# Attention and mixture of experts on one core: the order inside a group of value products, when inverses are read, how the groups are cut

## The chip, the cores and the metric

The kernel runs on one core of one Trainium2 chip. Its metric is the device time of one execution in microseconds (us). TensorE (PE) multiplies and transposes into PSUM, VectorE (DVE) and ScalarE (ACT) compute on SBUF and PSUM, GpSimd (POOL) and SyncE (SP) issue most of the DMA transfers. Each engine takes its own instructions in order; semaphores join them.

## The reference

One transformer layer on 2048 tokens of width 128: attention with 16 heads of width 64 under a causal mask, then a feed-forward part with one shared and eight routed experts, two of them for each token.

```python
x = x + attention(layernorm(x), qkv_w, qkv_b, out_w, out_b)
x = x + ffn(layernorm(x), gate_w, experts..., shared...)

# attention
qkv = einsum('bse,ehd->bshd', x, qkv_w) + qkv_b
q, k, v = split(qkv, 3)
logits = where(mask, einsum('bqhd,bkhd->bhqk', q, k) / sqrt(64), -0.7 * max)
probs = softmax(logits)
out = einsum('bhqd,hde->bqe', einsum('bhqk,bkhd->bqhd', probs, v), out_w) + out_b
```

Everything is fp32. The change lies in the attention part, which takes about the first 870 us of the profile.

## The kernel before

**Units of work.** The tokens are 16 blocks of 128. Heads are taken two at a time: eight pairs `j`. For each pair the query blocks are taken two at a time: eight values of `m`, in the order `turns = [2, 7, 0, 6, 1, 5, 3, 4]` (line 384). A step is one `(j, m)`; there are 64. Step `m` covers the query blocks 2m and 2m+1, here called rows 2m and 2m+1, and the key blocks 0 to 2m+1.

**Scores** (`score_units`, line 394). A row is worked in units of 512 keys: PE makes the scores of both heads into two PSUM tiles (line 429), DVE scales them, or adds the mask on the last unit, writes them to SBUF and takes the maximum on the way (lines 440 and 444: the eviction). After the last unit of a row DVE makes the negated maximum (`neg`), ACT takes the exponential of the row in place and its sum, once for each head (line 461). A row of m = 7 has four units, of m = 6 four, of m = 5 and 4 three, of m = 3 and 2 two, of m = 1 and 0 one. Scores are made ahead: a step with m >= 4 makes those of the step four places later, another step those of the step two places later.

**Turning the probabilities.** The value product needs the probabilities with keys on the partitions. For m < 4 PE transposes each 128x128 block (`turn`, line 522) and ACT copies it out of PSUM to `pT` (line 525). For m >= 4, called near steps in the code (`by_slabs(m)` is their number of key blocks turned this way), only the last two or four key blocks go that way, into `tail` (`turn_last`); the rest goes by slabs: DVE transposes a whole row of one head in 32x32 squares (line 496, 1536 columns for m = 7 and 6, 1024 for m = 5 and 4), SP issues four DMAs that write it to a DRAM buffer `stage` (line 500), and when all four slabs of the step are there one DMA reads the 3 or 2 MB back as `turned` (`load_turned`, line 514).

**One buffer for the rows of near steps.** The two rows of every near step, q = 0 and q = 1, lie in two SBUF tiles with one buffer each (line 413: the tag is `row7_0` or `row7_1`, `bufs=1`). So the first eviction of row 10 waits until everything has read row 12, its forerunner in the same tile: the exponentials, the transposes of `turn_last`, the slab transposes and the `stage` DMAs. The rows of q = 0 follow each other as 14, 12, 10, 8, those of q = 1 as 15, 13, 11, 9, round after round.

**When slabs and inverses are done.** After a row's exponentials, two entries (one a head) go into the queue `to_turn` with an age of 2 (line 464). Each group of work below begins with `turn_slabs(1)`, which lowers every age by one and does at most one slab if the first entry's age is below zero; later in the group `turn_slabs(1, age=False, due=True)` does one more that is due. When the last entry of a row is taken, DVE takes the reciprocals of the sums (line 480); when both rows of a step are through, it transposes them (line 483) and POOL writes them to DRAM (`invd`, line 485). `load_turned` does first whatever slabs of its step are left.

**Values and projection.** `times_v` (line 554) accumulates the value product of both heads over the key blocks in one of two PSUM tiles `av`; `spread` reads the inverses back over 64 partitions each (`inb`, line 567, four issues by POOL); `divide` multiplies the two on DVE into `aT` (line 575); `project` multiplies by the output weights on PE (`po`, line 581) and DVE adds to the residual `xr` (line 582).

**The loop** (lines 665 to 730). Each step is cut in groups of key blocks: a near step in its tail and two halves of the slab part, another step in threes (m = 3: 3, 3, 2; m = 2: 3, 3; m = 1: 3, 1; m = 0: 2). A group of a step with m < 4 is: one unit of `fill` (the next pair's projections, lines 352 and 369), slabs, the turns of this group (in the first group `spread` too), the projection of a finished step, the value products of the group before, `divide` if they end a step, slabs that are due, score units. A near group is the same with its own value products at once and `fill` after them. The score units of a near step with six or eight units are put as 3, 3, rest behind its three groups. There are 20 groups a pair. In the last pair the same loop also moves the routing of the feed-forward part on, one piece a group (`route_on`).

**What sets the order.** PE and DVE keep the order of the program text (`manual_schedule`). The order on ACT, POOL and SP is made by the scheduler. PSUM has six buffers with the tag `r`, used in turn by scores (two a unit), transposes, projections and `fill`, and two for `av`.

## Time and profile before

| what | value |
|---|---|
| median of 3 runs | 1049.83 us (1049.36 to 1052.5) |
| the profiled execution | 1043.9 us, span 1042.2 us |
| mean granted TensorE clock | 0.971 |
| PE busy | 949.6 us, 91% of the span |
| DVE busy | 745.1 us, 71% |
| ACT busy | 541.3 us, 52% |
| POOL busy | 211.3 us, 20% |
| HBM traffic | 105.10 MB read, 99.35 MB written |
| `stage` DMAs of a 1536-column slab | 192 KB each, four a slab, median 3.8 us to landing |
| `turned` DMA of m = 7 and 6 | 3072 KB, median 10.7 us to landing |

The profile is of one execution. A busy share is an average over stages; matmul ends are modelled, so a long matmul entry can hold a wait. In a timeline line the columns are start (us from the span's start), length in us, engine, source line, operation, tiles, shapes, count, and in brackets the idle time of the engine before it and what ended it. In a table of windows each line is a stretch of time, its length, the busy time (and instruction count) of PE, weight loads, DVE, ACT and POOL in it, the granted TensorE clock, the mean busy share of the DMA engines and GB/s.

### The profile page before, as it was taken

What the parts mean: (1) busy time and instruction counts of PE and PEld (TensorE: products, weight loads), DVE (VectorE), ACT (ScalarE), POOL (GpSimd) and SP (SyncE); (2) the same over time, 40 slices, a digit from 0 to 9 for tenths busy, and PEclk for the clock granted to TensorE, in tenths of its full rate; (3) what the DMA queues carried; (4) which work ended last, traced back from release to release, by engine and by line L of the source; (5) the groups of instructions that cost most, each with busy time, mean ns of one, the idle gap of its engine ahead of it and who ended that gap; (6) DMA issues with size and microseconds to landing.
All of it is one profiled execution on the core that took longest, in us unless ns stands there. A gap on an engine that the chain in (4) does not pass through costs nothing. (4 is left out here: it accounts for less than half of the span.)

```text
span 1042.2 us, 18362 instructions
## 1 busy us (share of the span) xinstructions
PE 949.6 (91%) x5928; PEld 573.3 (55%) x5928; DVE 745.1 (71%) x2315; ACT 541.3 (52%) x1015; POOL 211.3 (20%) x404
## 2 busy tenths in 40 slices
PE   4987999999999999999999999999999788689995
PEld 2553545565556556555555555556555446357773
DVE  3764788778877877887778777876787675545553
ACT  4552546655655565456556554655465452315551
POOL 1030110121102111111111111111111112734441
PEclk9988999999999999999999999999999898889998
DMA  9996748774787478747866875677577751443104
GB/s 200 190 275 172 272 117 308 251 215 144 258 277 213 160 245 272 210 165 252 257 189 190 253 245 174 204 250 243 165 221 254 250 172 65 142 129 85 43 26 125
DMA packets 126736, 205.33 MB, mean 197 GB/s; under 512 B 16449, under 2 KB 119203, under 8 KB 122545
## 3 DMA queue, kind: packets, MB, share of 16 engines
q1 hardware_dynamic: 116496, 190.06, 59.9%
q0 software_dynamic: 8416, 13.82, 5.4%
q8 instruction: 48, 0.79, 0.3%
q10 hardware_dynamic: 1728, 0.27, 0.2%
q14 instruction: 48, 0.39, 0.1%
HBM read 105.10 MB, written 99.35 MB: 196 GB/s over the span
## 5 line engine op out<-in xcount | busy, mean ns | idle before, releaser
L461 ACT ACTIVATE row<-row,neg 128x1920 f32<-128x1920 f32 (+15 forms) x256 | 306.3, 1202 | 255.0 <-DVE neg L458 115.2
L440 DVE TENSOR_SCALAR_CACHE_REDUCE row<-sc 128x512 f32<-128x512 f32 x384 | 243.2, 684 | 97.9 <-PE sc L429 68.2
L429 PE MATMUL sc<-kT,qT 64*128 64x512 f32 (+3 forms) x1280 | 299.4, 557 | 14.1 <-DVE row L440 5.9
L429 PEld LDWEIGHTS sc<-kT,qT 64*128 64x128 f32 x1280 | 128.3, 188 | 149.9 <-issue 79.9
L496 DVE STREAM_TRANSPOSE row<-row 128x1024 f32<-128x1024 f32 (+1 forms) x128 | 190.3, 1490 | 0.8 <-ACT row L461 0.8
L554 PE MATMUL av<-turned,vt 128*64 128x256 f32 x1280 | 158.0, 395 | 0.0
L485 POOL DMA_DIRECT2D invd<-inv x64 | 46.0, 718 | 506.3 <-DVE inv L483 503.1
L444 DVE CUSTOM_DVE_ANT_0 row<-sc,mask 128x384 f32<-128x384 f32 (+3 forms) x256 | 114.8, 485 | 19.6 <-PE sc L429 19.0
L554 PEld LDWEIGHTS av<-turned,vt 128*64 128x64 f32 x1280 | 88.7, 140 | 63.5 <-issue 24.6
L522 PE MATMUL tr<-ident,row 128*128 128x128 f32 x896 | 119.2, 276 | 3.3 <-ACT pT L525 1.9
L522 PEld LDWEIGHTS tr<-ident,row 128*128 128x128 f32 x896 | 99.6, 141 | 36.3 <-issue 19.0
L567 POOL DMA_DIRECT2D inb<-invd x128 | 76.1, 603 | 146.0 <-DMA invd<-inv 133.4
L525 ACT COPY pT<-tr 128x512 f32<-128x512 f32 (+1 forms) x160 | 79.0, 553 | 31.9 <-PE tr L522 31.9
L554 PE MATMUL av<-pT,vt 128*64 128x256 f32 (+1 forms) x640 | 79.6, 372 | 6.4 <-ACT pT L525 6.1
L352 PE MATMUL pq<-xnT,wq 128*128 128x512 f32 x128 | 72.0, 650 | 2.4 <-DVE row L440 2.4
L581 PE MATMUL po<-wo,aT 128*128 128x128 f32 x256 | 44.2, 297 | 26.0 <-DVE row L440 19.7
L554 PEld LDWEIGHTS av<-pT,vt 128*64 128x64 f32 x640 | 38.7, 136 | 47.9 <-issue 18.3
L581 PEld LDWEIGHTS po<-wo,aT 128*128 128x128 f32 x256 | 34.7, 197 | 44.1 <-DVE row L440 36.3
L525 ACT COPY tail<-tr 128x512 f32<-128x512 f32 x96 | 43.6, 520 | 16.7 <-PE tr L522 16.7
L949 POOL DMA_INDIRECT ybuf<-yo,to x39 | 38.3, 982 | 62.2 <-ACT yo L948 59.1
L461 ACT ACTIVATION_READ_ACCUMULATOR row<-row,neg 128x1 f32 x256 | 49.7, 194 | 0.0
L575 DVE TENSOR_TENSOR aT<-av,inb 128x256 f32<-128x256 f32 x64 | 26.5, 415 | 27.5 <-DMA inb<-invd 15.2
(169 smaller groups left out, 894.9 us busy)
## 6 DMA issues: line engine op xcount, KB each, us to landing
stage<-row SPq DMA_DIRECT2D x256, 192.0 KB, 3.8
turned<-stage SPq DMA_DIRECT2D x16, 3072.0 KB, 10.7
stage<-row SPq DMA_DIRECT2D x256, 128.0 KB, 2.6
turned<-stage SPq DMA_DIRECT2D x16, 2048.0 KB, 8.8
zbuf<-mask SPq DMA_DIRECT2D x8, 1056.0 KB, 19.2
inb<-invd POOLq DMA_DIRECT2D x128, 64.0 KB, 3.4
zs<-zbuf SPq DMA_DIRECT2D x39, 66.0 KB, 1.9
yt<-ybuf SPq DMA_DIRECT2D x4, 512.0 KB, 4.3
```

Of the source, the lines that this page charges most:

```text
L352: nc.tensor.matmul(pq, wq_of[j][:, s, :, :], xnT[:, ts(n, 512)], start=True, stop=True,)
L429: nc.tensor.matmul(sc[:, :cw], qT[i // 4][hd, ts(i % 4, P)], keys, start=True, stop=True)
L440: nc.vector.tensor_scalar(dst, src, SCALE, None, ALU.mult, ALU.max, accum_out=mh)
L444: nc.vector.tensor_tensor_reduce(out=rows[:, h, c0 : c0 + cw], in0=scs[h][:, :cw], in1=mask[:, 512 - cw : 512], scale=SCALE, scalar=-F32_M ...
L461: nc.scalar.activation(row, row, AF.Exp, bias=neg[:, h : h + 1], accum_out=sums[:, h : h + 1])
L485: nc.gpsimd.dma_start(invd_of[j, m].rearrange("n (a i) -> a n i", a=4), inv,)
L496: nc.vector.transpose(row, row)
L522: nc.tensor.transpose(tr[:, h, ts(q, P)], rows_of[j, m][q][:, h, ts(b, P)], ident)
L525: nc.scalar.copy(dst[:, :, q0 * P :], tr[:, :, q0 * P :])
L554: nc.tensor.matmul(av_of[j, m][hd, q0 * P :], vt[:, b, hd], pT[:, h], start=(b == near), stop=(b == (near or 2 * m + 2) - 1),)
L567: nc.gpsimd.dma_start(inb[h * D : (h + 1) * D, :].rearrange("d (q p) -> d q p", q=2), row.partition_broadcast(D),)
L581: nc.tensor.matmul(po[:, q, :], aT[:, ts(q, P)], wo[:, j, :], start=True, stop=True)
```

## The change

Five things are changed together.

1. The loop goes over a flat list of groups. A group now begins with its own value products; the turns of a group with m < 4 are made one group earlier, behind the value products of that group. The order inside is: slabs, (projection of a finished step if this group ends a step), value products, `divide` or else the projection, routing, due slabs, the next group's turns, one `fill` unit, `spread` of the next step, tails, `load_turned`, scores.
2. `spread` is put one group earlier, at the end of the step before. Rows of steps with m < 4 enter `to_turn` with age 1 instead of 2, and taking such an entry no longer counts against the one slab.
3. m = 2 is one group of six blocks, m = 3 two of four, m = 1 two of two: 18 groups a pair instead of 20.
4. Score units of a near step are put as 3, rest, 3 behind its three groups; a step of two groups has half behind each.
5. In the routing of the last pair the transposes of all its rows are one piece instead of one piece for each four.

No instruction's shape and no count of them changes. In the built program the DVE order around the step m = 7 of a pair is now: evictions of rows 0 and 1, slab of row 12, `xr` of m = 2, slab of row 12, eviction of row 10, two slabs of row 13, inverses of m = 6 and m = 0, `aT` of m = 7, eviction of row 11, slab of row 10. Before it was: two slabs of row 12, evictions of rows 0 and 1, slab of row 13, `aT` of m = 2, inverses of m = 6, slab of row 13, eviction of row 10, `xr` of m = 2, eviction of row 11, inverses of m = 0, `aT` of m = 7, slab of row 10.

```diff
--- before.py
+++ after.py
@@ -335,8 +335,11 @@
                     )
                     no_order("sent", ins)
 
-        turns = [lambda t0=t0: turn_row(t0) for t0 in range(0, n, 4)]
-        return [statistics, normed, None, *turns, None, logits, None, best1, best2, ranks]
+        def turn_rows():
+            for t0 in range(0, n, 4):
+                turn_row(t0)
+
+        return [statistics, normed, None, turn_rows, None, logits, None, best1, best2, ranks]
 
 
     attn = tc.tile_pool(name="attn", bufs=2)
@@ -461,7 +464,7 @@
                     nc.scalar.activation(
                         row, row, AF.Exp, bias=neg[:, h : h + 1], accum_out=sums[:, h : h + 1]
                     )
-                to_turn.extend([j, m, q, h, sums, 2] for h in range(2))
+                to_turn.extend([j, m, q, h, sums, 2 if X else 1] for h in range(2))
 
             units += [lambda c=c, unit=unit: unit(c) for c in range(nch)]
         return units
@@ -473,7 +476,9 @@
 
         for t in to_turn:
             t[-1] -= age
-        while to_turn and (to_turn[0][-1] < 0 or not (age or due)) and most:
+        while to_turn and (to_turn[0][-1] < 0 or not (age or due)):
+            if not most and by_slabs(to_turn[0][1]):
+                break
             j, m, q, h, sums, _ = to_turn.popleft()
             if h == 1:
                 inv = inv_of[j, m]
@@ -625,7 +630,6 @@
         u()
         turn_slabs(2)
     fill, later = deque(), deque()
-    last = []
     ending = None
 
     shared_w = []
@@ -662,73 +666,91 @@
                     blocks = [b for m in batch for b in (2 * m, 2 * m + 1)]
                     routes.append(deque(route_units(blocks)))
 
-    for n, (j, m) in enumerate(steps):
+    def groups_of(m):
+
+        near, width = by_slabs(m), 2 * m + 2
+        if near:
+            return [range(near, width), range(near // 2), range(near // 2, near)]
+        step = {2: 2, 4: 2, 6: 6, 8: 4}[width]
+        return [range(k, k + step) for k in range(0, width, step)]
+
+    def runs_of(m, units):
+
+        if by_slabs(m):
+            return [3, units - 6, 3]
+        return [units] if m in (0, 2) else [units // 2, units // 2]
+
+    groups = [(n, k, g) for n, (_, m) in enumerate(steps) for k, g in enumerate(groups_of(m))]
+
+    def turned_group(i):
+        n, _, group = groups[i]
+        return [turned(*steps[n], b) for b in group]
+
+    now = turned_group(0)
+    spread(*steps[0])
+    for i, (n, k, group) in enumerate(groups):
+        j, m = steps[n]
+        near = by_slabs(m)
         at = n % NM
-        if at == 0 and j + 1 < NP:
-            qkv[j + 1] = qkv_units(j + 1)
-
-
-            _, q, k, v = qkv[j + 1]
-            fill.extend([*k, q[3], *v])
-            later.extend([q[1], q[0], q[2]])
-            if j + 2 < NP:
-                load_wq(j + 2, nc.sync)
-            while j and blank:
-                nc.sync.dma_start(blank.popleft(), mask[:, :ROW].unsqueeze(1).to_broadcast([P, 16, ROW]))
-        if at == 0 and j == NP - 1:
-            load_shared()
-        if at == 5 and later:
-            assert not fill
-            fill.extend(later)
-            later.clear()
-        if at == 6 and j + 1 < NP:
-            assert not fill
-        near = by_slabs(m)
-        coming = scores_of(n + (4 if near else 2))
+        if k == 0:
+            if at == 0 and j + 1 < NP:
+                qkv[j + 1] = qkv_units(j + 1)
+
+
+                _, q, key, v = qkv[j + 1]
+                fill.extend([*key, q[3], *v])
+                later.extend([q[1], q[0], q[2]])
+                if j + 2 < NP:
+                    load_wq(j + 2, nc.sync)
+                while j and blank:
+                    clear = mask[:, :ROW].unsqueeze(1).to_broadcast([P, 16, ROW])
+                    nc.sync.dma_start(blank.popleft(), clear)
+            if at == 0 and j == NP - 1:
+                load_shared()
+            if at == 5 and later:
+                assert not fill
+                fill.extend(later)
+                later.clear()
+            if at == 6 and j + 1 < NP:
+                assert not fill
+            coming = scores_of(n + (4 if near else 2))
+            runs = runs_of(m, len(coming))
+            if n == 0:
+                coming.extend(scores_of(3))
+                runs = [len(coming)]
+        turn_slabs(1)
+
+        before, ending = ending, None
+        ends = group[-1] == (near or 2 * m + 2) - 1
+        if before is not None and ends:
+            finish(*before)
+        for t in now if not near else turned_group(i):
+            times_v(*t, qkv[j][0][2])
+        if ends:
+            ending = (j, m, divide(j, m))
+        elif before is not None:
+            finish(*before)
+        route_on()
+        turn_slabs(1, age=False, due=True)
+        if i + 1 < len(groups) and not by_slabs(steps[groups[i + 1][0]][1]):
+            now = turned_group(i + 1)
+        if fill:
+            fill.popleft()()
+        if i + 1 < len(groups) and groups[i + 1][1] == 0:
+            spread(*steps[n + 1])
+        if near and k == 0 and n + 2 < len(steps):
+            turn_last(*steps[n + 2])
+        if n == 0 and k == 0:
+            turn_last(*steps[1])
         if n == 0:
-            coming.extend(scores_of(3))
-
-        if near:
-            groups = [list(range(near, 2 * m + 2))]
-            groups += [list(range(k, k + near // 2)) for k in range(0, near, near // 2)]
-            runs = [3, 3, len(coming) - 6]
-        else:
-            groups = [list(range(k, min(k + 3, 2 * m + 2))) for k in range(0, 2 * m + 2, 3)]
-            half = len(coming) // 2
-            runs = {1: [len(coming)], 2: [2 * (half // 2), half], 3: [0, half, half]}[len(groups)]
-        for k, group in enumerate(groups):
-            if fill and not near:
-                fill.popleft()()
-            turn_slabs(1)
-            now = [turned(j, m, b) for b in group]
-            if k == 0:
-                spread(j, m)
-            if ending is not None:
-                finish(*ending)
-                ending = None
-            route_on()
-            ready, last = (last + now, []) if near else (last, now)
-            for t in ready:
-                jt, mt, b = t[:3]
-                times_v(*t, qkv[jt][0][2])
-                if b == (by_slabs(mt) or 2 * mt + 2) - 1:
-                    assert ending is None
-                    ending = (jt, mt, divide(jt, mt))
-            if fill and near:
-                fill.popleft()()
-            turn_slabs(1, age=False, due=True)
-            if near and k == 0 and n + 2 < len(steps):
-                turn_last(*steps[n + 2])
-            if n == 0 and k == 0:
-                turn_last(*steps[1])
-            if n == 0 and k == 1:
-                load_turned(*steps[1])
-            if near and k == 1 and n + 2 < len(steps):
-                load_turned(*steps[n + 2])
-            for _ in range(runs[k] if k < len(groups) - 1 else len(coming)):
-                if coming:
-                    coming.popleft()()
-    assert not last
+            load_turned(*steps[1])
+        if near and k == 1 and n + 2 < len(steps):
+            load_turned(*steps[n + 2])
+        for _ in range(runs[k]):
+            if coming:
+                coming.popleft()()
+        if k == len(runs) - 1:
+            assert not coming
     finish(*ending)
     assert len(routes) == 2
     attn.__exit__(None, None, None)
```

## The prediction

> **What bounds the kernel now.** I read the page's busy table first, then stretches of one pair in the table of windows, then the timelines of DVE and PE where two stretches that do the same work differ in length.
>
> ```profile
> PE 949.6 (91%) x5928; PEld 573.3 (55%) x5928; DVE 745.1 (71%) x2315; ACT 541.3 (52%) x1015; POOL 211.3 (20%) x404
> ```
>
> PE is the bound on the whole. From one pair to the next it takes about 101.4 us (slabs of row 14 start at 357.77 and 459.13), and DVE's instructions for a pair add up to some 84 us of that, so DVE may idle 17 us a pair before it binds. But a pair does not always run at PE's pace. The next table holds the same work twice, from the tail products of m = 7 to the scores behind the first group of m = 6: in the first pair, and in the fourth.
>
> ```profile
> 75.00:117.00 42.00, 32.17 (x186) 17.85 (x183) 25.97 (x65) 18.16 (x32) 4.93 (x10) 0.92 0.74 240
> 390.00:420.00 30.00, 28.76 (x190) 17.67 (x186) 23.05 (x62) 15.71 (x34) 4.79 (x9) 1.00 0.81 260
> ```
>
> The work is the same to a few instructions, the time 42 against 30 us. Cut in fives, the first pair shows why: DVE does nothing at all in two of the slices, while the DMA engines are at 0.95 and 0.91.
>
> ```profile
> 75.00:80.00 5.00, 3.96 (x30) 2.31 (x28) 4.38 (x10) 4.59 (x6) 0.73 (x1) 1.00 0.95 397
> 80.00:85.00 5.00, 2.22 (x12) 0.78 (x8) 0.00 (x0) 0.38 (x2) 1.32 (x3) 1.00 0.95 276
> 85.00:90.00 5.00, 2.54 (x12) 1.75 (x14) 3.30 (x11) 0.00 (x0) 0.00 (x0) 0.68 0.13 46
> 90.00:95.00 5.00, 5.00 (x24) 2.25 (x21) 4.30 (x8) 3.02 (x5) 0.73 (x1) 0.63 0.33 69
> 95.00:100.00 5.00, 5.00 (x34) 2.58 (x36) 0.00 (x0) 0.68 (x1) 0.12 (x1) 1.00 0.91 242
> ```
>
> DVE's timeline of that pair names the wait: the slab of row 12 ends, and the eviction of row 10, which goes into the same SBUF tile, idles 7.25 us until the slab's DMAs have landed; then row 13 and row 11 do it again.
>
> ```profile
> 77.70 1.75 DVE L496 STREAM_TRANSPOSE row<-row 128x1536 f32<-128x1536 f32 x1
> 86.70 0.69 DVE L440 TENSOR_SCALAR_CACHE_REDUCE row<-sc 128x512 f32<-128x512 f32 x1 [7.25 <-DMA stage<-row]
> ...
> 92.63 1.74 DVE L496 STREAM_TRANSPOSE row<-row 128x1536 f32<-128x1536 f32 x1
> 101.13 0.69 DVE L440 TENSOR_SCALAR_CACHE_REDUCE row<-sc 128x512 f32<-128x512 f32 x1 [6.76 <-DMA stage<-row]
> ```
>
> In the fourth pair the same distance, 387.25 to 395.23, is 7.98 us, but DVE fills it with rows 0 and 1, the slabs of row 13 and a division, and idles 0.85 us:
>
> ```profile
> 385.50 1.75 DVE L496 STREAM_TRANSPOSE row<-row 128x1536 f32<-128x1536 f32 x1
> 390.00 1.77 DVE L496 STREAM_TRANSPOSE row<-row 128x1536 f32<-128x1536 f32 x1
> 395.23 0.69 DVE L440 TENSOR_SCALAR_CACHE_REDUCE row<-sc 128x512 f32<-128x512 f32 x1 [0.85 <-DMA stage<-row]
> 401.71 0.69 DVE L440 TENSOR_SCALAR_CACHE_REDUCE row<-sc 128x512 f32<-128x512 f32 x1 [2.46 <-PE sc L429]
> ```
>
> PE shows what that is worth to the end. In the first pair it idles because the six PSUM tiles hold scores that DVE has not read.
>
> ```profile
> 75.00 1.68 PE L554 MATMUL av<-tail,vt 128*64 128x256 f32 x16
> 87.46 1.23 PE L581 MATMUL po<-wo,aT 128*128 128x128 f32 x4 [5.24 <-DVE row L440]
> 88.61 5.29 PE L554 MATMUL av<-turned,vt 128*64 128x256 f32 x24
> ...
> 116.72 0.71 PE L581 MATMUL po<-wo,aT 128*128 128x128 f32 x4 [0.48 <-DVE row L440]
> ```
>
> ```profile
> 390.22 1.68 PE L554 MATMUL av<-tail,vt 128*64 128x256 f32 x16
> 396.75 2.81 PE L554 MATMUL av<-turned,vt 128*64 128x256 f32 x24
> 419.39 0.71 PE L581 MATMUL po<-wo,aT 128*128 128x128 f32 x4 [1.24 <-DVE row L440]
> ```
>
> From the tail products to the last projection: 116.72 - 75.00 = 41.72 us against 419.39 - 390.22 = 29.17 us, 12.55 us apart.
>
> **The change, part by part.** I work against the profiled execution's own 1043.9 us; the median of the runs, 1049.83, is 0.6% above it.
>
> *Six blocks in one group, scores as 3, rest, 3.* Ages fall once a group. Row 12 is finished behind the second group of m = 4. Before, four groups followed until row 10's eviction (third of m = 4, two of m = 2, first of m = 7) and its slabs came due in the second of m = 2. Now m = 2 is one group, so they come due in the first group of m = 7, and in DVE's order nothing but row 12's own slab stands right ahead of row 10. Row 13's two slabs come behind row 10, and ahead of row 11 stand only two inverses and one division (0.7 us). That is the first pair's pattern, now in every pair. DVE's chain from the start of row 12's first slab: slab, `xr`, slab 3.75 us; wait 7.25; row 10 3.6 (86.70 to 90.31); two slabs 3.7; wait 6.76 (the inverses inside it); row 11 3.8: 28.9 us. In the fourth pair it took 21.9 us (383.77 to 405.66) and began 6.4 us ahead of the tail products; now it begins about 1 us behind them, once the evictions of rows 0 and 1 are through. So row 11 is out of PSUM about 30 us after the tail products begin, not 15.4. PE meanwhile has 17.4 us of work until it needs a tile of row 11 (products of m = 7, 7.2 us; six score units, 5; projection, turns, `fill`, 5.2) and waits for the rest. What follows row 11 (slabs of row 10, rows 2, 3 and 8, tails of m = 5) took 11.8 us in the first pair. Bounds: row 11's scores now stand one group later than in the first pair, which could hide one run of products with its turns, 3.6 us, so from below 8.9; from above, row 12's transfers meet the 3 MB read of m = 7 (10.5 us from issue to landing at 375.16) and the inverses of m = 0 come late as well, 17. I take 12.5 us, the nearest row. It counts for pairs two to seven, 6 x 12.5 = 75. The first pair pays already. The last pair paid 31.4 us for this stretch (795.22 to 826.67), with 6.07 us of DVE idle for the inverses of m = 0; it goes to about 41.5, +10.
>
> *Rows 14 and 15 to rows 12 and 13.* m = 3 has two groups instead of three, so these slabs come nearer to their successors too. All sixteen stage DMAs took 17 us from the first slab (357.77) to the last landing; DVE has about 15 us of work in between. New wait 1 to 2.5 us a pair on DVE, partly behind PE's products.
>
> *Values first, turns behind them.* Removed: PE's wait for the copies `pT` (0.98 us once a pair at m = 2, 6.1 us in the windows 100 to 800) and part of its waits at a projection, which no longer stands right behind three score units except in m = 0 and m = 2 (7.4 us in the same window). Added: the last four blocks of m = 3 are copied by ACT behind row 15's exponentials (2.02 + 2.00 us, then 2.0 us of copies); from row 15's scores on, ACT needs about 10.1 us and PE 8.2, so PE waits about 2 us a pair. The six copies of m = 2 stand behind row 12's exponentials (2 x 1.68), another 0.8. With the item above I take +1.5 us a pair over the rest of the pair, bounds -4 (all six microseconds of stalls there go, nothing comes but half the ACT wait) and +5: 7 x 1.5, about +10.
>
> *Inverses a step ahead.* In the steady pairs DVE waited about 2 us for `inb` of m = 0 (9.1 us in five waits), because `invd` was issued at 406.35 behind the `turned` read of 401.46. Now it goes out with that of m = 6, before the read; but the division follows in its own group. POOL is 20% busy and its four issues take 2.4 us; nothing else waits behind them. Gain at most 2 us a pair, inside a stretch that the chain above sets: 0. On SP the stage DMAs of row 12 now stand behind the read of m = 7, which waits for row 15's landing first; SP has been free of it by then (10 us): 0, and in the upper bound above.
>
> *Routing in ten pieces, 18 groups in the last pair.* The same pieces end in the same group; one more piece of the second batch is done in the loop: -1 (0 to -3).
>
> Sum: 1043.9 + 75 + 10 + 10 - 1 = 1138.
>
> The granted clock after such a wait: 0.68 and 0.63 in the windows 85 to 95, and 24 value products took 5.29 us instead of 2.81. In the first pair that loss lies inside DVE's chain, so it is 0 in my sum. [...]
>
> **The rivals.**
> *Faster.* The wait is covered: PE runs ahead into `av`, which has its own PSUM tiles, and the gains remain (0.98 + 1 + 2 us a pair): 1043.9 - 7 x 4 = 1016. It decides this way if DVE idles less than about 2 us ahead of row 10. Against it stands DVE's order and the 5.24 us that PE lost in the first pair.
> *Half.* DVE waits, but PE's lost time is only about 6 us a pair, since one of the two waits is covered by the later place of row 11's scores and the other gains come in: 1044 + 7 x 6 = 1086.
> *Worse.* Transfers are the bound: stage, `turned` and `inb` meet, 17 to 18 us a pair: 1044 + 7 x 18 = 1170.
> *No change.* What the order gives and takes cancels: 1044 to 1050.
>
> **How the numbers follow.** My case 0.71, half 0.12, worse 0.12, faster 0.04, no change 0.01. Time 1140. The range, 1088 to 1175, holds my own case with both ends of its bounds and about half of the two cases beside it; what is left out are the cases of 0.05 at the fast end and the outer halves of the others. Faster by over 0.3%, about what a measurement of this kernel can tell, 0.04; within it 0.01; slower 0.95.
>
> **What would show it.** Right: DVE's wait `row <- DMA stage<-row` grows from 27.0 us to over 100 us; ahead of row 10 it idles 6 to 8 us in each pair; the pair lasts 113 to 117 us; PE idles ahead of the `fill` unit between the value halves of m = 7 and ahead of the projection of m = 7; HBM traffic is unchanged. `av <- ACT pT` waits move from m = 2 to m = 3. Wrong: if slabs of row 12 end more than 8 us before row 10's first eviction, or if PE has idled under 5 us where DVE waited 14.

## The result, and the profile after

The changed kernel takes 1178.36 us (median of 4 runs, 1176.81 to 1180.09); the kernel before, timed beside it, 1050.87. The ratio is 1.121 (95% interval 1.119 to 1.124). The forecast was 1140 with 1088 to 1175: right in sign and in its main mechanism, too low by 38 us, and the result lies 3 us beyond its range. The runs timed beside each other are 127.5 us apart; the profiled execution took 1177.42 us (span 1175.7), 133.5 us above the one before.

Where these 133.5 us lie is read from the PE timelines. I cut each pair at two places that stand in both kernels: the first tail product of m = 7, and the first product of m = 6 on the slab part. From the one to the other is "the stretch", from there to the next pair's tail products "the rest". The "first expert product" is PE's first work on an expert's block (`pz`). The forecast column has the prediction's terms.

| part of the run | before, us | after, us | difference | forecast |
|---|---|---|---|---|
| start to the first pair's tail products | 75.0 | 72.7 | -2.3 | 0 |
| pair 1: stretch + rest | 42.4 + 71.7 | 43.6 + 76.2 | +5.8 | +1.5 |
| pairs 2 to 7: stretch | 176.9 | 244.0 | +67.1 | +75 |
| pairs 2 to 7: rest | 429.3 | 465.4 | +36.1 | +9 |
| last pair, tail products of m = 7 to the last projection | 84.7 | 100.9 | +16.2 | +10 |
| last projection to the first expert product | 46.8 | 60.4 | +13.6 | -1 |
| experts to the end | 115.5 | 112.4 | -3.1 | 0 |

The busy table of the page, whose columns are as in the line shown of the kernel before:

```profile
PE 998.2 (85%) x5928; PEld 598.2 (51%) x5928; DVE 739.6 (63%) x2315; ACT 545.9 (46%) x1017; POOL 211.9 (18%) x404
```

No engine has more to do; PE's busy time is 49 us longer for the same 5928 products, at a mean granted clock of 0.939 instead of 0.971. The waits of the whole run (engine, line, what was waited for: us in total, times, longest) point at the cause; in the kernel before the first of these lines stood at 27.0 us in 7 waits, the second at 19.7 in 10:

```profile
DVE row L443 <- DMA stage<-row: 178.0, 35, 7.6
...
PE po L586 <- DVE row L443: 54.8, 15, 9.9
...
PE pq L355 <- DVE row L443: 24.5, 8, 4.0
```

DVE's timeline of the fourth pair shows where these waits stand:

```profile
432.72 1.75 DVE L501 STREAM_TRANSPOSE row<-row 128x1536 f32<-128x1536 f32 x1
440.80 0.69 DVE L443 TENSOR_SCALAR_CACHE_REDUCE row<-sc 128x512 f32<-128x512 f32 x1 [6.33 <-DMA stage<-row]
...
446.38 1.74 DVE L501 STREAM_TRANSPOSE row<-row 128x1536 f32<-128x1536 f32 x1
...
455.09 0.69 DVE L443 TENSOR_SCALAR_CACHE_REDUCE row<-sc 128x512 f32<-128x512 f32 x1 [6.18 <-DMA stage<-row]
...
460.82 1.22 DVE L501 STREAM_TRANSPOSE row<-row 128x1024 f32<-128x1024 f32 x1
...
470.72 0.69 DVE L443 TENSOR_SCALAR_CACHE_REDUCE row<-sc 128x512 f32<-128x512 f32 x1 [5.16 <-DMA stage<-row]
...
475.23 1.21 DVE L501 STREAM_TRANSPOSE row<-row 128x1024 f32<-128x1024 f32 x1
...
482.27 0.69 DVE L443 TENSOR_SCALAR_CACHE_REDUCE row<-sc 128x512 f32<-128x512 f32 x1 [5.16 <-DMA stage<-row]
```

Each pair of lines is a row's last slab and the first eviction into the same SBUF tile: row 12 and row 10, 13 and 11, 10 and 8, 11 and 9. The first two are what the prediction described; in the kernel before the same place idled 0.85 us. The other two, 5.16 us each, it had not priced. PE in the stretch of this pair:

```profile
434.86 2.81 PE L559 MATMUL av<-turned,vt 128*64 128x256 f32 x24
441.55 2.08 PE L355 MATMUL pq<-xnT,wq 128*128 128x512 f32 x2 [3.88 <-DVE row L443]
443.56 4.88 PE L559 MATMUL av<-turned,vt 128*64 128x256 f32 x24
...
455.85 0.71 PE L586 MATMUL po<-wo,aT 128*128 128x128 f32 x4 [2.96 <-DVE row L443]
```

and in the table of windows (start:end, length, busy time of PE, weight loads, DVE, ACT and POOL, granted clock, DMA share, GB/s):

```profile
433.48:438.48 5.00, 4.19 (x32) 2.02 (x28) 0.99 (x1) 0.00 (x0) 0.00 (x0) 1.00 0.93 233
438.48:443.48 5.00, 1.93 (x2) 0.50 (x2) 2.68 (x9) 0.00 (x0) 0.00 (x0) 0.75 0.25 73
443.48:448.48 5.00, 5.00 (x26) 2.69 (x26) 4.89 (x12) 3.70 (x5) 0.73 (x1) 0.57 0.27 58
448.48:453.48 5.00, 4.40 (x20) 1.87 (x20) 0.42 (x1) 1.55 (x3) 0.82 (x2) 1.00 0.94 236
453.48:458.48 5.00, 2.63 (x16) 1.44 (x18) 3.39 (x11) 0.00 (x0) 2.53 (x5) 1.00 0.70 213
```

This is the picture that the prediction drew from the first pair: DVE stands still twice while the DMA engines are at 0.93 and 0.94, and PE idles ahead of the `fill` unit and of the projection of m = 7. After the idle of 3.88 us the granted clock was 0.75 and 0.57 and 24 products took 4.88 us instead of 2.81; after that of 2.96 us it stayed at 1.00.

In the rest of this pair PE waited as follows, first in the kernel before (420.03:491.58, 71.55 us), then in the kernel after (469.33:547.39, 78.06 us):

```profile
PE av L554 <- ACT pT L525: 1.0, 1, 1.0
PE sc L429 <- ACT tail L525: 0.7, 1, 0.7
PE tr L522 <- ACT pT L525: 0.2, 1, 0.2
```

```profile
PE po L586 <- DVE row L443: 1.8, 1, 1.8
PE tr L527 <- ACT pT L530: 1.2, 1, 1.2
PE pq L355 <- ACT pT L530: 1.1, 1, 1.1
PE sc L432 <- DVE xr L587: 0.9, 1, 0.9
PE sc L432 <- DVE row L443: 0.8, 1, 0.8
PE pv L372 <- DVE row L443: 0.2, 1, 0.2
```

The waits for ACT's copies grow from 1.9 to 2.3 us, those for DVE from nothing to 3.7. The remaining 2.4 us stand inside PE's own entries, 71.92 us instead of 69.56 at a granted clock of 1.00 in both; a modelled entry can hold a wait, and the trace doesn't say for what.

### The profile page after: what moved, and what is told of

It reads as the page before. It is cut to its first block, busy times and chain, and to the rows that moved or that the text cites. A ratio compares the mean times of both kernels' runs of the same rounds, so it can differ in the third digit from the quotient of the medians.

```text
span 1175.7 us, 18345 instructions
## 1 busy us (share of the span) xinstructions
PE 998.2 (85%) x5928; PEld 598.2 (51%) x5928; DVE 739.6 (63%) x2315; ACT 545.9 (46%) x1017; POOL 211.9 (18%) x404
## 3 DMA queue, kind: packets, MB, share of 16 engines
HBM read 105.10 MB, written 99.35 MB: 174 GB/s over the span
## 5 line engine op out<-in xcount | busy, mean ns | idle before, releaser
L443 DVE TENSOR_SCALAR_CACHE_REDUCE row<-sc 128x512 f32<-128x512 f32 x384 | 243.0, 685 | 242.3 <-DMA stage<-row 178.0
L432 PE MATMUL sc<-kT,qT 64*128 64x512 f32 (+3 forms) x1280 | 319.1, 573 | 25.0 <-DVE row L443 11.2
L432 PEld LDWEIGHTS sc<-kT,qT 64*128 64x128 f32 x1280 | 142.7, 192 | 169.1 <-issue 51.0
L559 PEld LDWEIGHTS av<-turned,vt 128*64 128x64 f32 x1280 | 89.4, 141 | 77.1 <-issue 34.3
L355 PE MATMUL pq<-xnT,wq 128*128 128x512 f32 x128 | 79.0, 709 | 32.2 <-DVE row L443 24.5
L530 ACT COPY pT<-tr 128x512 f32<-128x512 f32 (+1 forms) x160 | 75.3, 547 | 65.2 <-PE tr L527 65.1
L586 PE MATMUL po<-wo,aT 128*128 128x128 f32 x256 | 49.7, 321 | 56.0 <-DVE row L443 54.8
L559 PEld LDWEIGHTS av<-pT,vt 128*64 128x64 f32 x640 | 42.5, 144 | 36.9 <-issue 17.4
L367 ACT ACTIVATE kT<-pq,bqk 128x512 f32<-128x512 f32 x32 | 21.7, 681 | 72.1 <-PE pq L355 72.0
```

The source lines that it names most:

```text
L355: nc.tensor.matmul(pq, wq_of[j][:, s, :, :], xnT[:, ts(n, 512)], start=True, stop=True,)
L432: nc.tensor.matmul(sc[:, :cw], qT[i // 4][hd, ts(i % 4, P)], keys, start=True, stop=True)
L443: nc.vector.tensor_scalar(dst, src, SCALE, None, ALU.mult, ALU.max, accum_out=mh)
L530: nc.scalar.copy(dst[:, :, q0 * P :], tr[:, :, q0 * P :])
L559: nc.tensor.matmul(av_of[j, m][hd, q0 * P :], vt[:, b, hd], pT[:, h], start=(b == near), stop=(b == (near or 2 * m + 2) - 1),)
L586: nc.tensor.matmul(po[:, q, :], aT[:, ts(q, P)], wo[:, j, :], start=True, stop=True)
```

## The experiments

All kernels compute the whole reference. Stretch and rest are means over pairs two to six; "wait" is DVE's wait `row <- DMA stage<-row` in the whole run; "routing" is the time from the last projection to the first expert product. The runs were made in five sets, each on one chip with its own runs of the kernel before (medians 1052.8, 1042.0, 1053.5, 1042.9 and 1043.6), so times are compared as ratios or pair by pair. Of each diff the lines that carry the experiment are shown; some also move the first `turned` read or the score units to fit the new groups.

| set | kernel | median, us | ratio to before (95%) | stretch | rest | wait | routing |
|---|---|---|---|---|---|---|---|
| - | before, profiled | 1043.9 | 1 | 29.4 | 71.9 | 27.0 | 46.8 |
| - | after | 1178.4 | 1.121 (1.119 to 1.124) | 40.7 | 77.5 | 178.0 | 60.4 |
| 1 | a_early | 1090.7 | 1.038 (1.031 to 1.046) | 31.4 | 75.5 | 29.4 | 60.3 |
| 1 | a_33 | 1127.7 | 1.072 (1.064 to 1.079) | 33.5 | 78.1 | 37.3 | 60.0 |
| 1 | a_sc33 | 1178.5 | 1.120 (1.113 to 1.127) | 41.4 | 77.9 | 123.3 | 60.7 |
| 1 | b_six | 1152.2 | 1.095 (1.088 to 1.102) | 41.4 | 75.2 | 97.5 | 59.1 |
| 2 | a_early33 | 1078.0 | 1.035 (1.032 to 1.037) | 28.9 | 77.1 | 41.1 | 47.8 |
| 2 | a_early_m3 | 1108.5 | 1.063 (1.060 to 1.066) | 31.7 | 78.9 | 24.7 | 46.4 |
| 2 | b_early | 1045.9 | 1.003 (1.002 to 1.005) | 29.1 | 73.0 | 25.8 | 45.6 |
| 2 | a_pad | 1163.5 | 1.117 (1.114 to 1.120) | 40.6 | 77.6 | 177.6 | 47.7 |
| 3 | b_late | 1212.1 | 1.150 (1.143 to 1.156) | 46.8 | 75.7 | 184.9 | 59.9 |
| 3 | b_inv | 1039.4 | 0.987 (0.982 to 0.992) | 28.3 | 71.2 | 25.9 | 60.6 |
| 3 | b_sc | 1049.3 | 0.996 (0.993 to 0.998) | 29.4 | 71.1 | 53.6 | 56.2 |
| 3 | a_33sc33 | 1130.6 | 1.074 (1.068 to 1.080) | 33.0 | 78.9 | 39.0 | 60.0 |
| 4 | b_all | 1136.8 | 1.088 (1.083 to 1.092) | 39.0 | 77.2 | 141.5 | 46.4 |
| 4 | a_early33sc33 | 1076.6 | 1.031 (1.028 to 1.035) | 30.6 | 74.9 | 18.5 | 47.7 |
| 4 | b_inv_pad | 1025.0 | 0.982 (0.979 to 0.986) | 28.2 | 71.2 | 24.9 | 45.7 |
| 4 | b_inv_sc_pad | 1034.2 | 0.991 (0.987 to 0.994) | 29.4 | 71.0 | 42.5 | 45.7 |
| 5 | b_inv2 | 1027.9 | 0.985 (0.982 to 0.988) | 28.3 | 71.2 | 28.7 | 46.9 |
| 5 | b_inv_pad2 | 1024.8 | 0.983 (0.980 to 0.985) | 28.1 | 71.2 | 23.9 | 45.7 |

### Is it the nearness of slab and eviction?

**a_early**, the kernel after with slabs one group earlier:

```diff
-                to_turn.extend([j, m, q, h, sums, 2 if X else 1] for h in range(2))
+                to_turn.extend([j, m, q, h, sums, 1] for h in range(2))
```

> The kernel after with one number changed: slabs of the near rows come due one group of turns earlier (age 1, not 2), everything else as it is. In VectorE's order row 12's slabs then stand ahead of the evictions of rows 0 and 1 and row 13's slabs, as in the kernel before, instead of right ahead of row 10's eviction. Theory (the time is set by evictions that wait for the landing of a slab they follow too closely, in the stretch of m = 7 and again ahead of rows 8 and 9): the wait row <- DMA stage<-row falls from 178 us to under 60, and both parts of the loss go, the 11 us a pair in the stretch and most of the 6 us in the rest: 1040 to 1070 us. Rival A (the rest of a pair is lost to the values-first order itself, ScalarE's copies behind the exponentials): only the stretch comes back, 7 x 11 us and the last pair's 8: about 1085 to 1095. Rival B (the transfers are the bound, whatever the order): the wait moves to another reader of the same bytes and the time stays above 1150.

Measured 1.038. The wait is back at 29.4 us with the same bytes moved, so rival B, transfers as the bound, falls. DVE around row 10 in the fourth pair:

```profile
402.92 1.75 DVE L501 STREAM_TRANSPOSE row<-row 128x1536 f32<-128x1536 f32 x1
...
406.06 1.77 DVE L501 STREAM_TRANSPOSE row<-row 128x1536 f32<-128x1536 f32 x1
...
408.37 1.74 DVE L501 STREAM_TRANSPOSE row<-row 128x1536 f32<-128x1536 f32 x1
410.94 0.69 DVE L443 TENSOR_SCALAR_CACHE_REDUCE row<-sc 128x512 f32<-128x512 f32 x1 [0.83 <-DMA stage<-row]
```

From the end of row 12's last slab to row 10's eviction it is still 6.3 us (404.67 to 410.94), but DVE fills them with two evictions and the slabs of row 13. The stretch is back at 31.4 us, but the rest only went from 77.5 to 75.5: the time is what rival A had forecast. Something besides these waits costs 3.6 us a pair there. (Beside the 2 us that are left in the stretch stands a wait of DVE of 3.09 us for `inb`; in the kernel before it was 1.97 us.)

**b_late**, the kernel before with slabs one group later. PE's order is the same, instruction for instruction:

```diff
-                to_turn.extend([j, m, q, h, sums, 2] for h in range(2))
+                to_turn.extend([j, m, q, h, sums, 3] for h in range(2))
```

> The kernel before with one number changed: slabs come due one group of turns later (age 3, not 2). The order of the work on PE is the same, instruction for instruction; only VectorE's order moves: row 12's slabs stand right ahead of row 10's eviction, row 13's ahead of row 11's, row 10's ahead of row 8's, row 11's ahead of row 9's, as in the kernel after. Theory (this nearness alone, with none of the change's parts, makes the loss): the stretch of m = 7 goes from 29.8 to 41 or 42 us in pairs two to seven and to 42 in the last, the rest of a pair from 71.5 to 73 to 75; the wait row <- DMA stage<-row to 130 to 180 us: 1044 + 6 x 12 + 10 + 7 x 2.5 = about 1143, 1125 to 1165. Rival (the nearness costs only together with fewer groups or values first): under 1080.

Measured 1.150, more than the theory's 1.08 to 1.12 and more than the whole change. DVE in its fourth pair:

```profile
442.58 1.76 DVE L496 STREAM_TRANSPOSE row<-row 128x1536 f32<-128x1536 f32 x1
450.52 0.69 DVE L440 TENSOR_SCALAR_CACHE_REDUCE row<-sc 128x512 f32<-128x512 f32 x1 [6.18 <-DMA stage<-row]
...
456.43 1.74 DVE L496 STREAM_TRANSPOSE row<-row 128x1536 f32<-128x1536 f32 x1
464.51 0.69 DVE L440 TENSOR_SCALAR_CACHE_REDUCE row<-sc 128x512 f32<-128x512 f32 x1 [6.35 <-DMA stage<-row]
```

So nearness, with no part of the change, makes a loss of this kind. It isn't quite nearness alone: the excess over the theory lies in the stretch, 46.8 instead of 42 us, for the edit delays the inverses too, and DVE waited 5.48 us for the `inb` of m = 0 there.

**b_early**, the other side of it: the same line of the kernel before with age 1.

```diff
-                to_turn.extend([j, m, q, h, sums, 2] for h in range(2))
+                to_turn.extend([j, m, q, h, sums, 1] for h in range(2))
```

> The kernel before with the slabs (and inverses) due one group of turns earlier, nothing else. Theory: in its steady pairs no eviction waits for a landing, so there is little to gain; the waits that it has, 27 us in 7 times, lie in the first pair and the last: -6 to +3 us against the kernel before. Rival (earlier slabs meet VectorE's other work or the exponentials that they need, and cost): +1 to +2 us a pair, 8 to 16 us slower. If the time of the kernel before is also set by the nearness of slabs, over 10 us faster.

Measured 1.003, 3.9 us slower. One group earlier gains nothing, one group later costs 15%: the kernel before stood just inside the edge.

### Which part of the change brings it about?

**b_six**, the kernel before with only the six blocks in one group:

```diff
-            groups = [list(range(k, min(k + 3, 2 * m + 2))) for k in range(0, 2 * m + 2, 3)]
+            size = 6 if m == 2 else 3
+            groups = [list(range(k, min(k + size, 2 * m + 2))) for k in range(0, 2 * m + 2, size)]
```

> The kernel before with one part of the change alone: the six blocks of m = 2 in one group (19 groups a pair instead of 20), the old order within a group, the old cut of the scores. VectorE's order then has row 12's slabs right ahead of row 10's eviction and row 13's slabs ahead of row 11's, as in the kernel after; rows 8 and 9 keep the order of the kernel before. Theory: the stretch of m = 7 grows by 10 to 13 us in pairs two to seven and by 8 to 10 in the last, and the rest of a pair stays at 71.5 us: 1050 + 6 x 11 + 8 = 1115 to 1135. Rival (the stretch is lost only together with the values-first order): under 1080.

Measured 1152, above the range. The stretch is 12.0 us longer, as the theory has it; the rest did not stay at 71.5 but went to 75.2. A wait of only 97.5 us (after: 178.0) costs four fifths of the whole loss.

All 16 of these waits stand ahead of rows 10 and 11; no eviction of row 8 or 9 waits. What lengthens the rest here is read from PE at the cut, in the fourth pair:

```profile
461.49 1.22 PE L581 MATMUL po<-wo,aT 128*128 128x128 f32 x4 [3.24 <-DVE row L440]
462.65 4.92 PE L554 MATMUL av<-turned,vt 128*64 128x256 f32 x24
```

```profile
460.75:465.75 5.00, 4.26 (x20) 2.71 (x22) 3.43 (x15) 1.78 (x3) 0.12 (x1) 0.50 0.49 112
```

PE idled 3.24 us at the end of the stretch, the granted clock fell to 0.50, and the first 24 products of the rest took 4.92 us instead of 2.81. In pairs two to seven they took 4.46 to 5.16 us, so 1.7 to 2.4 of the 3.3 us that the rest is longer stand in these slow products. Shortly ahead of that idle DVE had waited 3.96 us for the `inb` of m = 0.

**a_33**, the other way round: the kernel after with m = 2 in two groups of three.

```diff
-        step = {2: 2, 4: 2, 6: 6, 8: 4}[width]
+        step = {2: 2, 4: 2, 6: 3, 8: 4}[width]
```

(and the scores of rows 0 and 1 cut as before)

> The kernel after with m = 2 in two groups of three blocks again (scores of rows 0 and 1 cut as before, 2 units and the rest), nothing else undone: 19 groups a pair. Row 12's slabs get one group more ahead of row 10's eviction; rows 10 and 8 keep theirs (row 8's eviction still follows row 10's slabs by one group, row 9's follows row 11's). Theory: the wait of some 6.3 us ahead of row 10 goes, those ahead of row 11 shrinks by the overlap, those of about 5 us ahead of rows 8 and 9 stay: 6 to 9 us a pair back of the 17, so 1115 to 1135 us. If six blocks in one group were the whole cause (my prediction's main step): under 1090. If it were none of it: 1170 to 1180.

Measured 1127.7, in the theory's range: the stretch fell by 7.2 us, the rest stayed, though DVE's wait is down to 37.3 us. But the theory's reason for the rest falls. In the rest of the fourth pair (451.56:529.55) DVE waited as follows:

```profile
DVE row L443 <- PE sc L432: 7.1, 5, 3.4
DVE aT L580 <- PE av L559: 4.4, 2, 2.8
DVE qT L365 <- PE pq L355: 4.0, 2, 3.7
DVE row L443 <- PE tr L527: 2.0, 1, 2.0
DVE xr L587 <- PE po L586: 1.0, 2, 0.7
DVE row L447 <- PE sc L432: 0.3, 1, 0.3
DVE row L443 <- issue: 0.3, 1, 0.3
```

It waits for no landing there, and the rest still takes 78.0 us, as in the kernel after (78.1, with two such waits of 5.16). So this rest is long without landings.

**a_sc33**, the kernel after with the near scores cut 3, 3, rest:

```diff
-            return [3, units - 6, 3]
+            return [3, 3, units - 6]
```

> The kernel after with the score units of a near step cut 3, 3 and the rest again (row 11 one group earlier, row 9 as well), nothing else undone. Theory: row 10's eviction waits as in the kernel after, row 11's stands closer behind row 13's slabs, and row 9's closer behind row 11's slabs, but PE meets the waits earlier: within 10 us of the kernel after, 1168 to 1188. Rival (the place of the scores is what costs the 6 us in the rest of a pair): 7 x 6 us back, about 1135.

Measured 1178.5: no difference, though DVE waits 55 us less. PE meets the same delay elsewhere, 50.9 us in eight waits of the transposes for an eviction.

**b_sc**, that part of the change alone in the kernel before:

```diff
-            runs = [3, 3, len(coming) - 6]
+            runs = [3, len(coming) - 6, 3]
```

> The kernel before with the score units of the near steps cut 3, rest, 3 instead of 3, 3, rest, nothing else. In VectorE's order row 9's eviction then follows row 11's slabs with only an inverse and a division between, and row 11's stands one group later. Theory (nearness to slabs sets the time, wherever it comes about): a wait of 3 to 5 us ahead of row 9, of which PE loses 1 to 4 us a pair, and none in the stretch of m = 7: 1050 to 1075. Rival (the place of the scores is free, as between the kernel after and the same with 3, 3, rest): within 4 us of the kernel before; if it relieves PSUM, faster.

Measured 0.996, a small gain where the theory had a loss. The waits came (53.6 us; 2.72 and 2.52 us ahead of rows 8 and 9 in the fourth pair), PE did not lose by them.

**b_inv**, the inverses alone in the kernel before:

```diff
-                to_turn.extend([j, m, q, h, sums, 2] for h in range(2))
+                to_turn.extend([j, m, q, h, sums, 2 if X else 1] for h in range(2))
-        while to_turn and (to_turn[0][-1] < 0 or not (age or due)) and most:
+        while to_turn and (to_turn[0][-1] < 0 or not (age or due)):
+            if not most and by_slabs(to_turn[0][1]):
+                break
```

> The kernel before with the inverses alone read a step ahead: sums of the rows without slabs come due one group earlier, and an inverse may go out behind the last slab of a group. Theory: VectorE's wait for inb of m = 0, some 2 us a pair, goes, but the stretch is not set by it: -8 to +3 us against the kernel before. Rival: each pair gains the 2 us, -14; or an inverse that is due early makes VectorE wait for the exponentials' sums, +1 a pair.

Measured 0.987, the rival: 1.8 us a pair. DVE's wait for `inb` of m = 0, 1.97 us in the fourth pair of the kernel before, is gone: its inverse is issued 8.9 us behind the tail products of m = 7, not 16.1. This part of the change, alone, beats both kernels.

**b_all**, six blocks, score cut and inverses together in the kernel before (the diffs of b_six, b_sc and b_inv), without the values-first order.

> The kernel before with three parts of the change together: the six blocks in one group, the near scores cut 3, rest, 3, the inverses a step ahead. What is left out is the values-first order with its groups of two and four, and the routing in ten pieces. Theory (the parts add, and values first costs by itself): 1152 for the six blocks, -5 for the scores, -9 to -14 for the inverses: 1128 to 1142, with the rest of a pair at 71 to 74 us; the 36 to 50 us that are missing to the kernel after are values first. Rival (values first is free, the loss is nearness alone): 1165 to 1185.

Measured 1136.8, as forecast, but by luck: the rest is 77.2, not 71 to 74. So without values first the rest is as long as in the kernel after, though not made up alike: the granted clock in it is 0.94 to 0.96 in pairs two to six, in the kernel after 1.00. In the fourth pair DVE waits 5.37, 4.40, 5.39 and 3.42 us for landings, the last two ahead of rows 8 and 9, which don't wait in b_six; DVE's wait of 4 to 5 us a pair for the `inb` of m = 0, which b_six has, is gone. A pair is 116.2 us long, in b_six 116.6: what the score cut and the inverses each do to it is not separated.

### What does values first cost by itself?

**a_early33**, early slabs and m = 2 in threes (the diffs of a_early and a_33 together).

> Both repairs together: the kernel after with the slabs due one group earlier, and m = 2 in two groups of three. All four slabs of rows 12 and 13 then stand ahead of the evictions of rows 0 and 1, and one group more lies between them and row 10. With only the early slabs a pair took 106.4 us, 31.1 of them in the stretch of m = 7 and 75.3 in the rest, against 101.3, 29.8 and 71.55 in the kernel before. Theory (what is left in the stretch is still the nearness of row 13's slabs to row 11; what is left in the rest is the values-first order): the stretch goes to about 29.8, the rest stays at 75: 1090.7 - 7 x 1.3 = about 1081 us, 1075 to 1088. Rival (the group count itself, one turn of ageing and `fill` a group, makes the rest): the rest falls too and the time goes to 1060.

Measured 1078, in the theory's range, but partly by luck. The stretch, 28.9 us, is shorter than in the kernel before, as the theory has it; the rest is 77.1, 5 us longer than before and 1.6 longer than in a_early. The routing is 12.5 us shorter and the experts are 4 us longer than in a_early, for a reason given below, and the ratios, 1.035 and 1.038, do not differ clearly.

**a_early33sc33**, with the score cut undone too (and the diff of a_sc33).

> Values first with its groups of two and four, the inverses a step ahead and the routing in ten pieces, with slabs due one group earlier: the kernel after with the six blocks and the score cut undone and the slabs early. Theory (no eviction waits for a landing here, so what is left is values first): the stretch 28 to 30, the rest 75 to 77.5 us against 71.2 in the kernel before with the inverses alone: 1070 to 1090. Rival (it was nearness to the end): under 1055.

Measured 1076.6: the theory. Values first, its groups of two and four, the routing and the earlier slabs are what is left; against the kernel before with the inverses (28.3 and 71.2) a pair takes 2.3 us more in the stretch and 3.7 in the rest. Earlier slabs alone cost 1.1 us in the rest (b_early, 73.0 against 71.9). Over pairs two to six PE idles 3.0 us a pair in the rest for ACT's copies, in b_inv 1.6, and 1.2 us ahead of scores for an eviction, in b_inv not at all; its own entries are 1.0 us longer. So the copies account for some 1.4 of the 3.7 us.

**a_33sc33**, the same with the slabs of the kernel after (the diffs of a_33 and a_sc33).

> The kernel after with two parts undone, the six blocks in one group and the cut of the scores; what remains of the change is values first with the turns behind them, the inverses a step ahead, m = 1 and m = 3 in two groups each, and the routing in ten pieces. Theory (values first costs by itself, because between a group's turns and its values only one run of scores covers ScalarE's copies): the rest of a pair at 76 to 77 us instead of 71.5, the stretch at 30 to 34, and 10 to 13 us behind the last projection if ScalarE stands still there again: 1085 to 1110. Rival (what is left of the change is free or a gain): 1035 to 1055.

Measured 1130.6, 20 us above the range. The rest is 78.9 us, 7.7 more than in b_inv, again with no wait for a slab's landing in that of the fourth pair. In the stretch inverses came late besides: DVE waited 46.3 us for `inb` in nine waits, 5.92 of them in the fourth pair ahead of the division of m = 0:

```profile
442.11 0.42 DVE L580 TENSOR_TENSOR aT<-av,inb 128x256 f32<-128x256 f32 x1 [5.92 <-DMA inb<-invd]
```

**a_early_m3**, a_early with m = 3 in groups of 3, 3 and 2 and scores 0, half, half.

```diff
-        step = {2: 2, 4: 2, 6: 6, 8: 4}[width]
+        step = {2: 2, 4: 2, 6: 6, 8: 3}[width]
-        return [units] if m in (0, 2) else [units // 2, units // 2]
+        half = units // 2
+        return [units] if m in (0, 2) else [half, half] if m == 1 else [0, half, half]
```

> The kernel after with the early slabs, and the eight blocks of m = 3 in groups of 3, 3 and 2 (scores 0, half, half) as in the kernel before, m = 2 still in one group of six. Theory (of the 3.8 us a pair that the rest still loses with early slabs, about 2 to 3 lie in m = 3, where four blocks' copies queue behind row 15's exponentials: 1.32 us ahead of the transposes and 2.27 us in the scores of row 4, against 0.5 in the kernel before): the rest falls by 1.5 to 3 us a pair, 1090.7 - 8 x 2 = 1067 to 1079. Rival (those stalls only move to the next reader of the same copies, or the rest is lost in the score order): 1086 to 1094.

Measured 1108, the rest of a pair 3.4 us longer than in a_early instead of 2 shorter. The waits of PE have a line that no other kernel has at this size:

```profile
PE av L559 <- ACT pT L530: 27.0, 8, 3.8
```

Behind m = 3's first group no scores stand now, so the next group's values follow their own turns at once and PE waits 3.8 us for the copies, once a pair. In the kernel before the values came a whole group behind their turns, and m = 3's group without scores had no such wait. So values first needs a run of scores behind a group's turns to cover the copies. How much of its 3.6 us a pair comes from copies that one run does not cover (they stand behind exponentials on ACT) is not shown; no run takes values first apart from its groups of two and four.

### The stall in the routing

In the kernel after ACT stands still behind the last projection, while the expert weights load:

```profile
1039.02 0.59 ACT L786 ACTIVATE sg<-pg 96x512 f32<-96x512 f32 x1 [1.05 <-issue]
1053.00 1.09 ACT L786 ACTIVATE sg<-pg 128x512 f32<-128x512 f32 x2 [13.38 <-remote]
```

**a_pad**: 54 small copies on ACT in the last three pairs of the kernel after.

```diff
+        if j >= 5:
+            extra = small.tile([P, 1], F32, tag="extra", name=f"extra_{i}", bufs=1)
+            nc.scalar.copy(extra, mask[:, :1])
```

> The kernel after with 54 copies of one column on ScalarE added, one ahead of each group of turns in the last three pairs. They compute nothing that is used. In the kernel after, from the last projection to the first expert product 60.4 us pass, against 46.8 before, and ScalarE stands still for 13.4 us ahead of an activation (`sg` of the second last group) though its operands are there, while 3.3 MB of expert weights are loaded; the kernel with only the six blocks changed shows the same stall of 10 us with ScalarE's instructions in the very order of the kernel before. Theory (ScalarE has run out of instructions, and the next piece of its program waits in the queues behind the weights: where the pieces begin depends on how many instructions came before): with 54 more the stall moves away, -8 to -13 us: 1165 to 1171. Rival (the stall belongs to the weights' transfers, wherever the program is): 1177 to 1190, the stall at the same activation.

The stall was gone, the routing took 47.7 us, the time was 1163.5: the theory seemed right. But the ratio, 1.117 (1.114 to 1.120), overlaps that of the kernel after. **b_inv_pad** (60 such copies beside the inverses alone) and **b_inv_sc_pad** (with the score cut too) seemed to repeat it.

> The kernel before with the inverses a step ahead, and 57 to 60 copies of one column on ScalarE added, one ahead of each group in the last three pairs; they compute nothing that is used. The kernel with the inverses alone takes 99.3 us a pair instead of 101.0, and shows the stall of ScalarE in the routing, 15.7 us, 60.6 us from the last projection to the first expert product. Theory (ScalarE runs out of instructions while the weights load): the stall goes, 60.6 falls to 46 to 49, -12 us: 0.970 to 0.982 of the kernel before. Rival (the stall belongs to the weights' transfers): no change, 0.985 to 0.992.

> As the run with the inverses and the copies on ScalarE, and the near scores cut 3, rest, 3 besides, which alone took 0.4% off the kernel before. Theory (row 11's scores one group later leave PE more to do while VectorE waits; the parts add): 2 to 5 us below the run without the cut, 0.966 to 0.980 of the kernel before. Rival (with the inverses early the wait that the cut relieved is gone): equal to it within 2 us, or slower by the wait ahead of row 9.

Measured 0.982 and 0.991, routing 45.7 in both. (The score cut costs 0.9% here, the rival: with the inverses early the wait that it relieved is gone, and row 11 stands a group later, 29.4 against 28.2 us in the stretch.) To price the copies I ran the pair side by side:

> The kernel before with the inverses alone a step ahead, once more, beside the next run. Expected: 0.984 to 0.992 of the kernel before, ScalarE's stall of 13 to 16 us in the routing, 60 us from the last projection to the first expert product.

> The same with 60 copies of one column on ScalarE that compute nothing, one ahead of each group in the last three pairs. Theory (the stall is a matter of where ScalarE's program stands while the weights load): 8 to 13 us below the run without the copies, timed on the same chip. Rival (the executions that are timed do not have the stall that the profiled one shows): within 3 us of it.

Measured 0.985 and 0.983: no difference. And the stall is not in b_inv2, the very kernel that showed it as b_inv. First b_inv, then b_inv2:

```profile
894.35 0.59 ACT L766 ACTIVATE sg<-pg 96x512 f32<-96x512 f32 x1 [0.64 <-PE pg L758]
910.69 1.08 ACT L766 ACTIVATE sg<-pg 128x512 f32<-128x512 f32 x2 [15.75 <-remote]
```

```profile
893.24 0.59 ACT L766 ACTIVATE sg<-pg 96x512 f32<-96x512 f32 x1 [1.19 <-PE pg L758]
897.58 0.60 ACT L766 ACTIVATE sg<-pg 128x512 f32<-128x512 f32 x1 [3.74 <-PE pg L758]
```

My theory of the instruction's place falls; that ACT had run out of instructions no trace shows. In the table the stall goes with the set: all eight kernels of sets 1 and 3 have it (routing 56 to 61 us), none of the ten of sets 2, 4 and 5 (45 to 48), whatever the kernel. The kernel before was slower by 10 us in just the sets that have it. So it belongs to the chip, or to its condition then, not to the change; what it is stays open.

## Why the prediction was right, and where it was wrong

**The mechanism and the main term were right.** "Six blocks in one group" was given 12.5 us a pair, from the first pair of the kernel before. The stretch grew by 11.3 us (pairs two to six), 12.0 with that part alone; the last pair's by 7.5 instead of 10. DVE idled 6.3 us ahead of row 10, PE idled at the two places named, the waits for `stage` came to 178.0 us, HBM traffic is the same, 105.10 and 99.35 MB. Two signs failed: a pair lasted 118.2 us, not 113 to 117, and the waits `av <- ACT pT` did not move to m = 3 but went from 6.1 us to none; PE now waits for the copies ahead of transposes (8.5 us, 1.9 before) and `fill` units (7.8 us).

**Wrong: the term for the rest of a pair.** "I take +1.5 us a pair over the rest of the pair, bounds -4 and +5" is the step that failed: it measured 5.6 us, 36 instead of 9 us over six pairs. The 5.6 us also lie above the upper bound. What the runs showed in its place:

Values first, with its groups of two and four, is enough for the whole of it. With the slabs due as in the kernel after it lengthens the rest by 6.2 us (a_33 against the kernel before) or 7.7 (a_33sc33 against b_inv), and in the fourth pair of both no eviction in the rest waits for the landing of a slab. With the slabs a group earlier it is 3.6 us (a_early against the kernel before) or 3.7 (a_early33sc33 against b_inv). I had taken 2.8 us of ACT wait and let gains that did not come take part of it away. The mechanism named is the smaller part: PE's waits for ACT's copies grow by 1.4 us in a_early33sc33 and by 0.4 us in the fourth pair of the kernel after; the others are for DVE (3.7 us there) or stand inside PE's entries. Why the slabs' due time matters here without a wait for landings stays open.

"Rows 14 and 15 to rows 12 and 13" looked at the wrong rows. No eviction of row 12 or 13 waits in the fourth pair of the kernel after, and none over 2 us in the others; those of rows 8 and 9 wait 5.16 us each in the fourth pair, because everything behind row 11 comes late and so stands close again. That these waits lengthen the rest is not shown: the fourth pair of a_33 has as long a rest without them.

Without values first the rest can be long too: b_late, b_six and b_all have 75.7, 75.2 and 77.2. In b_six rows 8 and 9 do not wait either; there more than half of the increase stands in the 24 slow products behind the last idle of the stretch (4.92 us at a granted clock of 0.50 in the fourth pair). The two losses do not add: without values first (b_all) a pair took 116.2 us, with it 118.2. How the 5.6 us divide stays open. The first pair, whose stretch was long before, lost 4.5 us in its rest too.

**Wrong: the last pair and the routing.** Behind its stretch the last pair lost 8.7 us more, with the same waits ahead of rows 8 and 9 (5.58 and 5.18 us). "Routing in ten pieces: -1" met +13.6 - 3.1 us, but nearly all of that is not the change's: the trace of before happens to lack the stall of ACT that the trace of after has. Without it the two executions are about 123 us apart, and the kernel after with 54 small copies took 1163.5 us on a chip without the stall. On such chips the ten pieces gained nothing: kernels with them took 46.4 to 47.8 us for the routing, those without 45.6 to 46.9.

**Not tested as priced, and worth more alone: the inverses.** "Inside a stretch that the chain above sets: 0" has no run of its own; none takes the inverses out of the changed kernel. With the chain and the old inverses (b_six) DVE waits 4 to 5 us a pair for the `inb` of m = 0; with the new ones and the score cut (b_all) it does not, and the stretch is 2.4 us shorter, the rest 2.0 longer. In the kernel before, where the chain does not set the stretch, the same part is worth 1.8 us a pair.

**The rivals.** "Faster" fell with DVE's 6 us ahead of row 10, "half" with the stretch. "Worse", transfers as the bound, gave 1170, the nearest number, by a wrong mechanism: a_early moves the same bytes with the same buffers at 1.038.

**The clock.** The row was the place of the loss inside DVE's chain, price 0; a stretch of 11.3 us, below the 12.5 taken without it, fits that in the kernel after. It does not hold everywhere: in b_six 1.7 to 2.4 us a pair of slow products stand behind the stretch and lengthen the rest. The length of the last idle alone did not settle the granted clock: in the kernel after it was 0.57 after 3.88 us of idle and 1.00 after 2.96 in the fourth pair, and 1.00 after 3.31 in the sixth; in the kernel before it was 0.66 in the 5 us that followed 1.66 us of idle in the sixth pair (621.54:626.54), and 24 products took 4.50 us there.

**Besides.** DVE's instructions fill 80.3 us of a pair of the kernel before, not "some 84"; no term of the sum rests on it.

## What to carry to other kernels

When a due time is counted in steps of a loop, merging steps moves it in microseconds: measure the distance that a buffer needs from its last write-out to its next use, here 7.94 to 8.71 us from the start of a 1536-column slab to the eviction that waited for it (b_late and the kernel after, fourth pair), for every user of the buffer, those further down the chain too. A wait's total is not its price: 97.5 us of the same wait cost 100 us, 37.3 with another order 75, 53.6 nothing. Parts of a change are worth trying alone; here the smallest, the inverses a step ahead, takes the kernel before to 0.985 (0.982 to 0.988) by itself.

## What the runs showed of the hardware

One kernel, the same program, carried a stall of 15.75 us on ACT on one chip (b_inv) and none on another (b_inv2): routing 60.6 and 46.9 us. All eight kernels of the two sets with the stall have one of 11.5 to 15.8 us, and the kernel before differs by 1% between such sets, 1042.0 to 1053.5. A single profile of each kernel, taken apparently on two chips, had put 10 us of that down to the change; only the same kernel run twice showed it.

The granted clock was not settled by the length of the last idle alone: 1.00 after 3.31 us in the sixth pair of the kernel after, 0.66 after 1.66 us in the sixth pair of the kernel before.
